# Pairwise products of 32 fields on one core: output slots planned as a ring beside the tiles, upper fields first, a group's load in two pieces

## The chip, the core and the metric

The kernel runs on one core of one Trainium2 chip. The metric is the device time of that core in microseconds. Three runs of the kernel before gave a median of 1286.29 us (1286.14 to 1286.42). Beside them stands one execution under the hardware profiler, from which all rows of the profile come.

## The reference

```python
r_x: float32 (4096, 32, 64)          # batch, fields, embedding
W:   float32 (64, 64)
vid = einsum('bfd,de->bfe', x, W)
i, j = triu_indices(32, k=1)         # 496 pairs i < j
y = x[:, i, :] * vid[:, j, :]        # (4096, 496, 64)
```

Each field of each row of the batch is multiplied by one small matrix, and then, for each of the 496 pairs of fields, the raw left field is multiplied element by element by the transformed right field. The output has 520 MB, the input 33.6 MB.

## The kernel before, in words

**Tiles.** The host lays the batch out as 16 tiles of 256 rows. A tile holds 128 partitions (two halves of the batch tile by 64 embedding places) by 32 fields by 128 columns, so one field of one tile is 512 B in each of 128 partitions, 65,536 B in all, and one output pair has the same size. A *unit* is such a 512 B stretch. One SBUF tensor, `mem`, has 445 units in each partition; input tiles and output slots both live in it. The padding of the DRAM tensors' rows is never moved.

**TensorE.** For each half of a tile's fields (16 of 32) it waits for one count of the semaphore `free`, makes 4 matmuls of 512 columns against a block-diagonal copy of W (each shows as two in the profile) into PSUM (`vid`), and adds one to `there` (function `half`, L272). All tiles' products go into the same PSUM tensor, so a half may be overwritten only when VectorE has done with it; VectorE tells that by `free`.

**VectorE.** For each tile it runs through the 496 pairs in the order of `by_block` (L51): the 120 pairs inside the lower 16 fields, the 256 pairs of a lower with an upper field, the 120 pairs inside the upper fields. The order is cut into instructions by `products` (L67), where a pair run hits the end of an output slot or a seam in it. One instruction is one `tensor_tensor` multiply (L253) of 1 to 112 pairs. It adds one to `made`, or, where a half of PSUM has become free, one to `free` instead (L246 to L248); `owed` holds such a count back if the instruction ends a slot. What an instruction must wait for is worked out in `after` (L164): every transfer that reads units which it overwrites, and, for transfers, the count of `made` at which the last instruction that touched the units has ended. L178 puts that count down; for an instruction that tells `free` it is the next count of `made`.

**Slots.** `SLOTS` is a list written out by a planner: 70 slots of (pairs, first unit in `mem`, seams). The pairs of all 16 tiles, 7936 in one sequence, fill one slot after the other. A slot can span two tiles. When its last pair is made, its store is issued (L264). A seam is a place at which the ground under the slot becomes free at a different time; instructions are cut there.

**Transfers.** All go through SP's one queue, in the order in which the Python code issues them, each with its own semaphore: 11 loads and 70 stores. SP waits before it issues: a store for `made`, a load for the stores and the products that use its units.

**Loads.** Tile 0 comes first in two pieces, with W in front of its lower half. Then tiles 1 to 3 in one transfer and tiles 5 and 4 in two. `GROUPS` has two further groups, tiles 6 to 10 and 15 to 11, each of 160 fields in three pieces (`CUTS`), placed by `XPLACE`. L265 issues the next group's load when `t + 2 == loaded`: at the end of tile 4 for tiles 6 to 10, at the end of tile 9 for tiles 11 to 15. The first store after a group of loads also waits until the second-last piece has landed (`hold[-2]`, L261).

**TensorE's loops.** Tiles of a load run in one hardware loop; ahead of it TensorE waits for the load.

Of the kernel before, what the change touches and what calls it, by code (L numbers as in the profile page):

```python
# [12 lines left out]
C = 128  # L13

UNITS = 445


GROUPS = [
    [[0], [1, 2, 3], [5, 4]],
    [[6, 7, 8, 9, 10]],  # L20
    [[15, 14, 13, 12, 11]],
]
CUTS = [[None, [(0, 38), (38, 64)]], [(0, 127), (127, 134), (134, 160)], [(33, 160), (26, 33), (0, 26)]]
XPLACE = [317, 349, 381, 413, 32, 0, 285, 317, 349, 381, 413, 128, 96, 64, 32, 0]


SLOTS = [
# [10 lines left out]
]  # L38


PAD = 24
# [9 lines left out]
def by_block():  # L51


    def within(lo):
        yield "step", lo, 2, 1, 0
        for k in range(2):
            yield "step", lo, 4, 2, k
        for i in (lo, lo + 8):
            yield "row", i + 4, i, 4, 4
        yield "row", lo + 8, lo, 8, 8  # L60

    yield from within(0)
    yield "row", 16, 0, 16, 16
    yield from within(16)


def products(blocks, at=0):  # L67
# [60 lines left out]
        return instruction  # L128


def overlap(a, b):
    return a[0] < b[1] and b[0] < a[1]


def pairwise_bilinear_kernel(nc, x0, x, out):
    NT = sum(len(tiles) for group in GROUPS for tiles in group)
    F = x0.shape[1] - 1 - PAD0
    D = P // 2
    NP = F * (F - 1) // 2
    BANK = 512 // C  # L140
# [16 lines left out]
    def transfer(out_, in_, units, reads, needs):  # L157
        sem = nc.alloc_semaphore(f"moved{len(moved)}")
        sp.issue(lambda: nc.sync.dma_start(out=out_, in_=in_), needs).then_inc(sem, 16)  # L159
        sp.note(sem, 16)  # L160
        moved.append((units, reads, sem))
        return sem

    def after(units):  # L164

        needs = [(s, 16) for u, reads, s in moved if reads and overlap(u, units)]
        last = max((n for spans, n in worked if any(overlap(units, s) for s in spans)), default=0)
        return needs + [(made, last)] * (last > 0)
# [3 lines left out]
    def work(make, spans, needs, tells):  # L172
# [5 lines left out]
        worked.append((spans, counts[made] + (tells is free)))  # L178
        dve.note(tells, counts[tells])

    place = XPLACE[0]
    first = [
        transfer(
            mem[:, :, :].rearrange("p u c -> p (u c)")[:, place * C - D : (place + HALF) * C],
            x0.rearrange("p u c -> p (u c)")[:, C - D : (1 + HALF) * C],
            (place - 1, place + HALF), False, [],
        ),
        transfer(mem[:, place + HALF : place + F, :], x0[:, 1 + HALF : 1 + F, :], (place + HALF, place + F), False, []),
    ]
    work(lambda: nc.vector.memset(w2[:, :], 0.0), [], [], made)  # L190
    for half in (slice(0, D), slice(D, P)):
        work(
            lambda: nc.vector.tensor_copy(w2[half, half], mem[half, place - 1, C - D :]),  # L193
            [(place - 1, place)], [(first[0], 16), (made, 1)], made,
        )
    nc.vector.wait_ge(made, 3).then_inc(free, 1)
    nc.vector.wait_ge(first[1], 16).then_inc(free, 1)
    owed = 0

    loads = {0: first}  # L200
    loaded = 1

    def load(tiles, cuts):
        nonlocal loaded
        place = XPLACE[tiles[0]]
        at = (loaded - 1) * F
        loaded += len(tiles)
        sems = []
        for lo, hi in cuts or [(0, len(tiles) * F)]:
            units = (place + lo, place + hi)  # L210
            sems.append(transfer(mem[:, units[0] : units[1], :], x[:, at + lo : at + hi, :], units, False, after(units)))
        for t in tiles:
            loads[t] = sems
        return sems

    hold = []
    groups, cuts = iter(GROUPS), iter(CUTS)
    for tiles, parts in zip(next(groups)[1:], next(cuts)):
        hold = load(tiles, parts)

    for t in range(NT):
        xs = (XPLACE[t], XPLACE[t] + F)
        xt = mem[:, xs[0] : xs[1], :]
        blocks = list(products(by_block(), t * NP))
        for k, (at, m, w, i, di, j, dj) in enumerate(blocks):
            slot = bisect_right(STARTS, at) - 1
            n = m * w
            begin, end = STARTS[slot], STARTS[slot + 1]
            size, home = SLOTS[slot][:2]
            units = (home + at - begin, home + at - begin + n)  # L230
            ot = mem[:, home : home + size, :]
            o = mem[:, units[0] : units[1], :]
            if m == 1:
                left = xt[:, i : i + w, :]
                right = vid[:, j : j + 1, :].to_broadcast([P, w, C])
            else:
                o = o.rearrange("p (m w) c -> p m w c", m=m)
                right = vid[:, j : j + (m - 1) * dj + 1 : dj, :].unsqueeze(2).to_broadcast([P, m, w, C])
                if di == 0:
                    left = xt[:, i : i + w, :].unsqueeze(1).to_broadcast([P, m, w, C])  # L240
                else:
                    left = xt.rearrange("p (m d) c -> p m d c", d=di)[:, i // di : i // di + m, i % di : i % di + w, :]
            top = j + (m - 1) * dj
            low = top < HALF
            later = blocks[k + 1 : k + 2]
            owed += not later or low and later[0][5] + (later[0][1] - 1) * later[0][6] >= HALF  # L246
            tells = free if owed and at + n < end else made
            owed -= tells is free  # L248
            needs = [(there, 2 * t + 2 - low), *after(units)]
            if tells is free and t == 0:  # L250
                needs += [(s, 16) for s in loads[1]]
            work(
                lambda: nc.vector.tensor_tensor(o, left, right, ALU.mult),  # L253
                [units, (xs[0] + i, xs[0] + i + w + (m - 1) * di)],
                needs,
                tells,
            )
            at += n
            if at == end:
                needs = [(made, counts[made])]  # L260
                if hold:  # L261
                    needs.append((hold[-2], 16))
                    hold = []
                transfer(out[:, begin:end, :], ot, (home, home + size), True, needs)  # L264
        if t + 2 == loaded < NT:  # L265
            (tiles,) = next(groups)
            hold = load(tiles, next(cuts))

    for sem, n in sp.waits([(sem, 16) for _, _, sem in moved]):
        nc.sync.wait_ge(sem, n)  # L270
# [1 line left out]
    def half(xt, lo):  # L272
        nc.tensor.wait_ge(free, 1).then_inc(free, -1)  # L273
        for b in range(lo, lo + HALF, BANK):
            last = nc.tensor.matmul(vid[:, b : b + BANK, :], lhsT=w2[:, :], rhs=xt(b), start=True, stop=True)  # L275
        last.then_inc(there, 1)

    pe = Queue(nc.tensor, behind)
    runs = []
    for t in range(NT):  # L280
        step = XPLACE[t] - XPLACE[t - 1] if t else 0
        if runs and (t == 1 or loads[t] is loads[runs[-1][-1]]) and (len(runs[-1]) == 1 or step == XPLACE[runs[-1][1]] - XPLACE[runs[-1][0]]):
            runs[-1].append(t)
        else:
            runs.append([t])
    for run in runs:
        base = XPLACE[run[0]]
        if run[0]:
            for s, n in pe.waits([(s, 16) for s in loads[run[0]]]):
                nc.tensor.wait_ge(s, n)  # L290
        if len(run) == 1:
            for lo in (0, HALF):
                half(lambda b: mem[:, base + b : base + b + BANK, :], lo)
            continue
        step = XPLACE[run[1]] - base
        with nc.Fori(0, len(run), engines=[mybir.EngineType.PE]) as i:
            for lo in (0, HALF):
                half(lambda b: mem[:, bass.ds(i * step + (base + b), BANK), :], lo)
    ctx.close()


# [41 lines left out]
```

## Time and profile before

| | before |
|---|---|
| median of three runs | 1286.29 us (1286.14 to 1286.42) |
| the profiled execution | 1286.44 us, of which its span 1284.9 us |
| moved by DMA | 33.59 MB read, 520.09 MB written, 431 GB/s over the span |
| VectorE busy | 1084.1 us, 348 instructions, 345 of them products |
| TensorE busy | 187.7 us, 256 matmuls |
| VectorE idle ahead of products, until a store had landed | 163.4 us, 34 times |
| VectorE idle ahead of products, until TensorE was done | 7.1 us, once |

The span is the time between the first and the last instruction or event of the profiled execution; what lies around it, 1.54 us, is in the run's time and not in the trace. The page divides the span into 40 slices and gives for each the share of time in which the 16 DMA engines were busy, and the rate. The granted clock of TensorE has a mean of 0.57 in this execution.

### The profile page before, as it was taken

The numbers are of one execution on the slowest core, as the hardware profiler recorded it, in microseconds if no ns is written. First come the engines' busy times: TensorE is split into PE (matmuls) and PEld (weight loads), VectorE is DVE, ScalarE is ACT, GpSimd is POOL, SyncE is SP. The second block draws the span as 40 slices with busy tenths as digits, with TensorE's granted clock in tenths as the row PEclk, the third lists the DMA queues.
The fourth block names the chain that finished last, engine by engine and source line by source line (L and its number), as shares of the span: only waits on it lengthen the run. The fifth ranks groups of instructions, "written<-read, shape, count | busy, mean of one in ns | idle before, by whom it ended". The sixth has DMA issues, their size and how long they took to land.

```text
span 1284.9 us, 1195 instructions
## 1 busy us (share of the span) xinstructions
PE 187.7 (15%) x256; PEld 72.8 (6%) x256; DVE 1084.1 (84%) x348; POOL 0.2 (0%) x4
## 2 busy tenths in 40 slices
PE   3111021201021103021110211011202030212000
PEld 1000000100000001000000100000000010000000
DVE  6899998899967389899799993849998889999952
POOL 0000000000000000000000000000000000000000
PEclk8655555656566656555565555565557565565555
DMA  9999999999999999999999999999999999999998
GB/s 401 438 429 439 436 428 433 436 436 423 445 430 431 424 430 426 441 432 434 439 429 443 431 427 441 419 423 438 441 433 442 418 437 441 429 429 443 436 422 385
DMA packets 11668, 553.72 MB, mean 431 GB/s; under 512 B 1296, under 2 KB 1296, under 8 KB 1552
## 3 DMA queue, kind: packets, MB, share of 16 engines
q1 hardware_dynamic: 11664, 553.69, 99.8%
q14 instruction: 4, 0.03, 0.0%
HBM read 33.59 MB, written 520.09 MB: 431 GB/s over the span
## 4 chain that ended last, share of the span: by engine, by line
DMA 48%; DVE 48%; issue 2%; SPq 0%
DVE mem L253 48%; DMA out_dram<-mem 43%; DMA mem<-in_r_x_dram 5%; SPq L159 0%; SPq L124 0%
## 5 line engine op out<-in xcount | busy, mean ns | idle before, releaser
L253 DVE TENSOR_TENSOR mem<-mem,vid 128x1024 f32<-128x1024 f32 (+17 forms) x345 | 1083.5, 3213 | 170.5 <-DMA out_dram<-mem 163.4
L275 PE MATMUL vid<-mem,w 128*128 x256 | 187.7, 902 | 999.8 <-PEq L273 999.8
L275 PEld LDWEIGHTS vid<-mem,w 128*128 128x128 f32 x256 | 72.8, 299 | 1113.7 <-issue 1113.7
L193 DVE COPY w<-mem 64x64 f32<-64x64 f32 x2 | 0.4, 191 | 4.9 <-DMA mem<-in_r_x_dram 4.9
L190 DVE MEMSET w<- 128x128 f32 x1 | 0.2, 165 | 0.8 <-PEq L312 0.8
L312 POOL MEMSET const-bfloat16-1.0<- 128x1 bf16 x1 | 0.1, 102 | 0.0
L312 POOL MEMSET const-uint8-127<- 128x1 uint8 x1 | 0.1, 102 | 0.0
L312 POOL MEMSET const-float32-0.0<- 128x1 f32 x1 | 0.1, 99 | 0.2 <-issue 0.2
L312 POOL MEMSET const-float32-1.0<- 128x1 f32 x1 | 0.1, 99 | 0.0
## 6 DMA issues: line engine op xcount, KB each, us to landing
out_dram<-mem SPq DMA_DIRECT2D x15, 8128.0 KB, 27.5
out_dram<-mem SPq DMA_DIRECT2D x14, 7680.0 KB, 24.9
out_dram<-mem SPq DMA_DIRECT2D x6, 7168.0 KB, 26.2
out_dram<-mem SPq DMA_DIRECT2D x5, 7936.0 KB, 28.3
out_dram<-mem SPq DMA_DIRECT2D x3, 7424.0 KB, 22.6
out_dram<-mem SPq DMA_DIRECT2D x3, 5888.0 KB, 21.0
mem<-in_r_x_dram SPq DMA_DIRECT2D x2, 8128.0 KB, 37.9
out_dram<-mem SPq DMA_DIRECT2D x2, 8064.0 KB, 24.9
```

Of the source, the lines that this page charges most:

```text
L190: work(lambda: nc.vector.memset(w2[:, :], 0.0), [], [], made)
L193: lambda: nc.vector.tensor_copy(w2[half, half], mem[half, place - 1, C - D :]),
L253: lambda: nc.vector.tensor_tensor(o, left, right, ALU.mult),
L275: last = nc.tensor.matmul(vid[:, b : b + BANK, :], lhsT=w2[:, :], rhs=xt(b), start=True, stop=True)
L312: nc = _bacc.Bacc("TRN2", target_bir_lowering=False, num_devices=1, dynamic_dma_scratch_size=512)
```

## The change

The tiles now lie in units 0 to 192 of `mem`, downwards from `TOP`: the first tile of a group ends at unit 192, each further one lies 32 units lower (`place_of`). Slots lie beside and over the used tiles, in units 48 to 440, and were planned anew: 69, of up to 128 pairs (32 of them have 128; before 127 at most), with other places and seams. In a tile the pairs inside the upper 16 fields come first, then those across, then those inside the lower 16; TensorE makes the upper half first, and W stands behind the upper half of tile 0. Each group is loaded in two pieces (128 and 32 fields), so there are 8 loads and 69 stores, 77 transfers. The load of a group is now issued at the start of the group's first tile (before tile 6 and before tile 11). TensorE waits ahead of a group's loop for the pieces that hold the group's first tile; for the others VectorE waits, ahead of the instruction that gives TensorE its `free`.

```diff
+TOP = 192
 GROUPS = [
-    [[0], [1, 2, 3], [5, 4]],
-    [[6, 7, 8, 9, 10]],
-    [[15, 14, 13, 12, 11]],
+    (0, [(32, 160), (0, 32)]),
+    (6, [(64, 192), (32, 64)]),
+    (11, [(64, 192), (32, 64)]),
 ]
-CUTS = [[None, [(0, 38), (38, 64)]], [(0, 127), (127, 134), (134, 160)], [(33, 160), (26, 33), (0, 26)]]
-XPLACE = [317, 349, 381, 413, 32, 0, 285, 317, 349, 381, 413, 128, 96, 64, 32, 0]
...
+    (128, 304), (127, 192, 112), (113, 319), (64, 192), (96, 256, 63), (88, 352), (112, 192), (120, 304, 48),
...
+    (128, 192, 120), (120, 320), (72, 192), (96, 264, 56), (80, 360), (112, 192), (128, 304), (128, 160),
...
-    yield from within(0)
-    yield "row", 16, 0, 16, 16
     yield from within(16)
+    yield "row", 16, 0, 16, 16
+    yield from within(0)
...
+def place_of(t, fields):
+    first = max(begin for begin, _ in GROUPS if begin <= t)
+    return TOP - (t - first + 1) * fields
...
+    def load(g):
+        (begin, pieces), end = GROUPS[g], ends(NT)[g]
+        begin = max(begin, 1)
+        low = place_of(end - 1, F)
         sems = []
+        for lo, hi in pieces:
+            at = (begin - 1) * F + lo - low
+            sems.append(transfer(mem[:, lo:hi, :], x[:, at : at + hi - lo, :], (lo, hi), False, after((lo, hi))))
+            loads.append((range(begin, end), (lo, hi), sems[-1]))
         return sems
...
     for t in range(NT):
+        if t in begins[1:]:
+            hold = load(begins.index(t))
...
-            top = j + (m - 1) * dj
-            low = top < HALF
+            high = j >= HALF
             later = blocks[k + 1 : k + 2]
-            owed += not later or low and later[0][5] + (later[0][1] - 1) * later[0][6] >= HALF
+            owed += not later or high and later[0][5] < HALF
             tells = free if owed and at + n < end else made
             owed -= tells is free
-            needs = [(there, 2 * t + 2 - low), *after(units)]
-            if tells is free and t == 0:
-                needs += [(s, 16) for s in loads[1]]
+            needs = [(there, 2 * t + 2 - high), *after(units)]
+            if tells is free and t + 1 < NT and t + 1 not in begins:
+                needs += loaded(t + 1)
...
-        if t + 2 == loaded < NT:
-            (tiles,) = next(groups)
-            hold = load(tiles, next(cuts))
...
+    for begin, end in zip(begins, ends(NT)):
+        if begin:
+            for s, n in pe.waits(loaded(begin)):
+                nc.tensor.wait_ge(s, n)
```

The lines of the changed kernel that the prediction names: L188 puts down the count of `made` at which an instruction's units are free, L231 issues a group's load, L257 chooses between `free` and `made`, L264 is the product.

More of the change, by code (lines that the diff above doesn't have):

```diff
@@ L60, in within @@
         yield "row", lo + 8, lo, 8, 8
+    yield from within(16)
+    yield "row", 16, 0, 16, 16
     yield from within(0)
-    yield "row", 16, 0, 16, 16
-    yield from within(16)
 def products(blocks, at=0):
@@ L128, in issue, with ends @@
         return instruction
+def place_of(t, fields):
+    first = max(begin for begin, _ in GROUPS if begin <= t)
+    return TOP - (t - first + 1) * fields
+def ends(tiles):
+    return [begin for begin, _ in GROUPS[1:]] + [tiles]
 def overlap(a, b):
@@ L135, in pairwise_bilinear_kernel @@
 def pairwise_bilinear_kernel(nc, x0, x, out):
-    NT = sum(len(tiles) for group in GROUPS for tiles in group)
     F = x0.shape[1] - 1 - PAD0
+    NT = (x.shape[1] - PAD) // F + 1
     D = P // 2
@@ L179, in work @@
         dve.note(tells, counts[tells])
-    place = XPLACE[0]
+    place = place_of(0, F)
     first = [
         transfer(
-            mem[:, :, :].rearrange("p u c -> p (u c)")[:, place * C - D : (place + HALF) * C],
-            x0.rearrange("p u c -> p (u c)")[:, C - D : (1 + HALF) * C],
-            (place - 1, place + HALF), False, [],
+            mem[:, :, :].rearrange("p u c -> p (u c)")[:, (place + HALF) * C : (place + F) * C + D],
+            x0.rearrange("p u c -> p (u c)")[:, HALF * C : F * C + D],
+            (place + HALF, place + F + 1), False, [],
         ),
-        transfer(mem[:, place + HALF : place + F, :], x0[:, 1 + HALF : 1 + F, :], (place + HALF, place + F), False, []),
+        transfer(mem[:, place : place + HALF, :], x0[:, :HALF, :], (place, place + HALF), False, []),
     ]
@@ L192, in pairwise_bilinear_kernel @@
         work(
-            lambda: nc.vector.tensor_copy(w2[half, half], mem[half, place - 1, C - D :]),
-            [(place - 1, place)], [(first[0], 16), (made, 1)], made,
+            lambda: nc.vector.tensor_copy(w2[half, half], mem[half, place + F, :D]),
+            [(place + F, place + F + 1)], [(first[0], 16), (made, 1)], made,
         )
@@ L198, in pairwise_bilinear_kernel, with loaded @@
     owed = 0
[L200 to L207, printed above, removed]
-        sems = []
[L209 to L213, printed above, removed]
-        return sems
[L216 to L219, printed above, removed]
+    loads = [(range(1), (place, place + F + 1), sem) for sem in first]
+    def load(g):
+        (begin, pieces), end = GROUPS[g], ends(NT)[g]
+        begin = max(begin, 1)
+        low = place_of(end - 1, F)
+        sems = []
+        for lo, hi in pieces:
+            at = (begin - 1) * F + lo - low
+            sems.append(transfer(mem[:, lo:hi, :], x[:, at : at + hi - lo, :], (lo, hi), False, after((lo, hi))))
+            loads.append((range(begin, end), (lo, hi), sems[-1]))
+        return sems
+    def loaded(t):
+        units = (place_of(t, F), place_of(t, F) + F)
+        return [(sem, 16) for tiles, piece, sem in loads if t in tiles and overlap(piece, units)]
+    hold = load(0)
+    begins = [begin for begin, _ in GROUPS]
     for t in range(NT):
-        xs = (XPLACE[t], XPLACE[t] + F)
+        if t in begins[1:]:
+            hold = load(begins.index(t))
+        xs = (place_of(t, F), place_of(t, F) + F)
         xt = mem[:, xs[0] : xs[1], :]
@@ L278, in pairwise_bilinear_kernel @@
     pe = Queue(nc.tensor, behind)
[L279 to L289, printed above, removed]
-                nc.tensor.wait_ge(s, n)
[L291 to L298, printed above, removed]
+    for begin, end in zip(begins, ends(NT)):
+        if begin:
+            for s, n in pe.waits(loaded(begin)):
+                nc.tensor.wait_ge(s, n)
+        base = place_of(begin, F)
+        with nc.Fori(0, end - begin, engines=[mybir.EngineType.PE]) as i:
+            for lo in (HALF, 0):
+                half(lambda b: mem[:, bass.ds(base + b - i * F, BANK), :], lo)
     ctx.close()
@@ L318 @@
     x = x.reshape(2, NT, C, F, D).transpose(0, 4, 1, 3, 2).reshape(2 * D, NT, F, C)
-    x = x[:, [t for group in GROUPS for tiles in group for t in tiles]]
-    x0 = _np.pad(x[:, 0], ((0, 0), (1, PAD0), (0, 0)))
-    x0[:, 0, C - D :] = _np.concatenate([w, w])
-    x = _np.pad(x[:, 1:].reshape(2 * D, (NT - 1) * F, C), ((0, 0), (0, PAD), (0, 0)))
+    x0 = _np.pad(x[:, 0], ((0, 0), (0, 1 + PAD0), (0, 0)))
+    x0[:, F, :D] = _np.concatenate([w, w])
+    x = x[:, [t for (begin, _), end in zip(GROUPS, ends(NT)) for t in range(end - 1, max(begin, 1) - 1, -1)]]
+    x = _np.pad(x.reshape(2 * D, (NT - 1) * F, C), ((0, 0), (0, PAD), (0, 0)))
     arrays, args = {}, []
```

17 rows, old and new, of the table SLOTS are left out of this document.

## The prediction

> **What bounds the kernel now.** I read the page from the top: busy shares, then the slices of DMA, then the queue.
>
> ```profile
> span 1284.9 us, 1195 instructions
> PE 187.7 (15%) x256; PEld 72.8 (6%) x256; DVE 1084.1 (84%) x348; POOL 0.2 (0%) x4
> DMA  9999999999999999999999999999999999999998
> DMA packets 11668, 553.72 MB, mean 431 GB/s; under 512 B 1296, under 2 KB 1296, under 8 KB 1552
> q1 hardware_dynamic: 11664, 553.69, 99.8%
> ```
>
> The 16 DMA engines are busy 99.8% of the span: DMA is the bound, VectorE (84%) and TensorE (15%) are not. The change moves the same bytes (every product once, every field once), so time can only be won where DMA is slower than its best or idle, and is lost, microsecond for microsecond, wherever DMA runs dry. Next, by stages, the view of windows; its columns are the stretch, its length, busy time of PE, PEld, DVE, POOL, the granted clock, DMA share, GB/s.
>
> ```profile
> 0.00:1.70 1.70, 0.00 (x0) 0.00 (x0) 0.17 (x1) 0.20 (x4) 1.00 0.00 0
> 380.00:388.00 8.00, 3.83 (x5) 1.76 (x6) 4.17 (x3) 0.00 (x0) 0.50 0.91 392
> 388.00:426.00 38.00, 1.81 (x4) 0.46 (x3) 29.99 (x10) 0.00 (x0) 0.59 0.98 419
> 430.00:770.00 340.00, 54.32 (x72) 21.05 (x72) 305.74 (x103) 0.00 (x0) 0.57 1.00 435
> 900.00:1200.00 300.00, 47.82 (x64) 18.43 (x64) 279.49 (x91) 0.00 (x0) 0.57 1.01 435
> 1281.00:1284.50 3.50, 0.00 (x0) 0.00 (x0) 0.00 (x0) 0.00 (x0) 0.50 0.09 37
> 1284.50:1284.90 0.40, 0.00 (x0) 0.00 (x0) 0.00 (x0) 0.00 (x0) 0.50 0.00 0
> ```
>
> Between loads DMA moves 435 GB/s, share 1.00, so one pair (128 partitions x 512 B = 65,536 B) costs 65,536 / 435 = 0.151 us; 128 pairs 19.3 us, 32 pairs 4.8 us. DMA is at rest only for 1.7 us at the start and about 3 us at the end. A group's load comes with no rest: 0.98 of share at 419 GB/s. How before manages that is in the chain of work that ended last (start, length, what):
>
> ```profile
> 355.60 32.00 DMA out_dram<-mem
> ...
> 387.62 0.34 SPq L159
> ...
> 388.01 38.76 DMA mem<-in_r_x_dram
> 426.77 0.02 issue
> 426.79 0.02 SPq L124
> 426.80 0.03 issue
> 426.83 19.28 DMA out_dram<-mem
> 446.11 0.03 issue
> 446.14 12.96 DVE mem L253 x3
> ```
>
> The second group's load is issued at 387.6, behind the 22nd store, after 2464 pairs by the sums of SLOTS. Tile 6, which needs it, begins at pair 2976 (6 x 496): 512 pairs of lead, mostly tile 5. VectorE multiplies tile 5 while the load runs, and at 426.83, when its second-last piece has landed, two finished stores go out at once. That lead is what the change takes away.
>
> **The change part by part: the load's place.** Before, L265 issues a group's load once the tile two short of the loaded ones is done, one whole tile ahead. After, L231 issues it at the start of the tile that reads it. In the built program of the changed kernel SP's order is: store of slot 24, load of 128 fields, load of 32 fields, store of slot 25; and again store of slot 46, two loads, store of slot 47. Slot 25 holds pairs 2935 to 3048: 41 of tile 5 and 72 of tile 6, so it can't go out before tile 6 is multiplied, and tile 6 waits for the load. Slot 47 (5432 to 5552) has 24 pairs of tile 10 and 96 of tile 11. SP issues in order, so nothing else can fill DMA. Prices of the steps in between:
>
> ```profile
> L253 DVE TENSOR_TENSOR mem<-mem,vid 128x2048 f32<-128x2048 f32 x76 | 171.0, 2279 | 24.8 <-DMA out_dram<-mem 24.8
> L253 DVE TENSOR_TENSOR mem<-mem,vid 128x1024 f32<-128x1024 f32 x101 | 117.4, 1212 | 40.2 <-DMA out_dram<-mem 33.1 <-PE vid L275 7.1
> L253 DVE TENSOR_TENSOR mem<-mem,vid 128x5120 f32<-128x5120 f32 x4 | 21.9, 5481 | 7.3 <-DMA out_dram<-mem 7.3
> L253 DVE TENSOR_TENSOR mem<-mem,vid 128x896 f32<-128x896 f32 x2 | 2.2, 1079 | 0.0
> ```
>
> A product of 8 pairs (1024 elements) is 1.21 us, of 16 pairs 2.28, of 40 pairs 5.48, of 7 pairs 1.08.
>
> ```profile
> 5.90 0.41 DVE L193 COPY w<-mem 64x64 f32<-64x64 f32 x2 [4.91 <-DMA mem<-in_r_x_dram]
> 6.69 10.07 PE L275 MATMUL vid<-mem,w 128*128 x16 [6.69 <-PEq L273]
> 13.37 32.33 DVE L253 TENSOR_TENSOR mem<-mem,vid 128x1024 f32<-128x1024 f32 x10 [7.06 <-PE vid L275]
> 88.28 5.11 PE L275 MATMUL vid<-mem,w 128*128 x8 [52.93 <-PEq L273]
> 432.06 5.59 PE L275 MATMUL vid<-mem,w 128*128 x8 [42.25 <-PEq L273]
> ```
>
> Half a tile on TensorE takes 5.1 us (at 88.28) to 6.7 (6.69 to 13.37, from rest); after a rest of over 100 us I take 6.3 with the hand-over to VectorE. From landing to TensorE's start lies between the 0.02 us with which SP follows a landing (426.77) and the 0.79 from 5.90 to 6.69, which contains two copies; I take 0.5.
>
> ```profile
> 0.73 0.38 SPq L159
> ```
> ```profile
> mem<-in_r_x_dram SPq DMA_DIRECT2D x1, 1056.0 KB, 5.1
> ```
>
> From an issue to its first packet: the first load is issued at 0.73 and DMA moves nothing until 1.7, so 1.0 us. From the last packet to its landing: 0.4, the dead end of the span. Together 1.4; the whole 1056 KB load takes 5.1 us against 2.5 for its bytes at 435 GB/s, so at most 2.6. I take 1.4 and keep 2.6 for the range.
>
> By the Trainium skill, page "DMA: Bandwidth & Descriptors", section "Anatomy of one DMA — SWDGE (gpsimd) path", the fixed part of a DMA is about 2.0 us, most of it the receipt of the last write. It is stated for GpSimd's queue, and this trace shows 1.4 to 2.6 for SP's; by it the four turnarounds below would cost 0.6 us more each, an estimate of 1324.
>
> *Stop A, tile 6.* The load's first piece lands; 0.5 to TensorE, 6.3 for the upper half, then 72 pairs in six products of 8, 8, 8, 16, 16, 16: 3 x 1.21 + 3 x 2.28 = 10.5. With 1.4 that is 18.7 us, while DMA has 32 pairs left: 4.8. DMA rests **13.9 us**.
>
> *Stop B, tile 11.* The second piece (fields 32 to 64) overwrites tile 10, and must wait for its last reader. That product tells its end on `free` (L257), so L188 puts down the next count of `made`, 204, and in the built program it is tile 11's first product that makes 204. So the second piece waits for the first to land, for TensorE and for one product: 1.4 + 0.5 + 6.3 + 1.2 = **9.4 us** with nothing in the queue. Behind it stands slot 47's store, which needs five more products (8, 8, 16, 16, 40): 2 x 1.21 + 2 x 2.28 + 5.48 = 12.5, against the piece's 4.8. Both ends have the same issue delay: another **7.7 us**.
>
> **The ring.** In the new plan a slot may lie on the ground of the one just before, which has to land first: by comparing places this is so twice. The last 15 of slot 24's pairs (8 and 7) and the last 8 of slot 46's. There the queue holds nothing behind the store being waited for: 1.4 + 1.21 + 1.08 = **3.7 us**, and 1.4 + 1.21 = **2.6 us**. Before has one such place (slot 44 on 43), with the third group's load queued between the two. For the other slots: a pair costs VectorE 0.13 us (2279 - 1212 ns for 8 pairs more) and each product 0.15, against 0.151 a pair for DMA, so VectorE gains back about 1.5 us a slot of 128 pairs in five products and a stop isn't followed by others.
>
> **Order of fields, fewer pieces.** Upper half first: 376 of a tile's 496 pairs read the upper products (j of 16 and over), 120 the lower, before as after; TensorE refills one half in 5 to 7 us behind at least 16 us of products on the other. Nothing; without that cover 6 us a tile. VectorE has 314 products for 345: 31 x 0.15 = 4.6 us off an engine that doesn't bound. DMA: 8 loads for 11. In before, the stretch from 380 to 426 loses 8 x (1 - 392/435) + 38 x (1 - 419/435) = 2.2 us against 435 GB/s, twice 4.4 in all. Part is the mixing of loads and stores, which stays: between 0 and 4.4 gained, I take 1.5. At the start the same five microseconds lead to the first product; the first store, 48 pairs, goes behind a 32-field piece (4.8 us; before 26 fields), and 144 pairs are multiplied about 21 us after 13.4, before that store ends. Nothing.
>
> ```profile
> out_dram<-mem SPq DMA_DIRECT2D x15, 8128.0 KB, 27.5
> ```
>
> **Rows of 64 KiB.** 32 stores and 3 loads have rows of 65,536 B, none had before (127 pairs at most). The nearest rows are the 15 stores of 127 pairs (8128 KB), inside the 435 GB/s windows: nothing. Bound on the other side: 419 GB/s as in the load stage.
>
> **Sum.** 13.9 + 9.4 + 7.7 + 3.7 + 2.6 - 1.5 = 35.8 us on the span of 1284.9: 1320.7. Around its span the profiled execution has 1286.44 - 1284.9 = 1.54: 1322.2, and it lies 0.15 over the median of the runs (1286.29): **1322**.
>
> **The rivals.**
> *Faster: DMA never runs dry.* Place: the two group changes. It decides by whether finished stores of 120 pairs (18.7 us) stand behind the load, as two did at 426.83. Price: no stop, the pieces' 0 to 4.4 us gained, about 1284. For it: 84% of VectorE, and before's own load. Against it: SP's order above leaves no finished store behind the load. Chance 0.04. By the same page and section, at 2.0 us a transfer, four transfers fewer would give 8 us, an estimate of 1278; this trace has packets back to back (share 1.00), which speaks against it.
> *Stop A hidden.* Place: tile 6 alone. It decides by whether slot 25's 113 pairs are multiplied before the load's last piece has gone by, 72 of them in 4.8 us. Price: 13.9 us less, 1308. Against it: ten and a half microseconds of products and 6 of TensorE stand in the way. Chance 0.04.
> *64 KiB rows at 419 GB/s.* 35 transfers of 19.3 us, 4% longer each: 26 us more, 1348. It would show in windows with no load. Chance 0.07.
> *The change doesn't do what it says:* the slots don't fit the free ground and VectorE waits at each; then small dips all over, 1335 to 1350. Chance 0.03.
>
> **How the numbers follow.** Forecast 0.82. Its own range: TensorE 5.1 to 6.7 in two stops (-2.4, +0.8), landing to TensorE (-1, +0.6), the pieces (-2.9, +1.5), turnaround up to 2.6 in four stops (+4.8): 1316 to 1329.7. The rivals lie outside with 0.18. Range 1315 to 1330. Faster 0.02, same 0.02 (within 0.2%, 2.6 us, about what measurements of this kernel can tell apart), slower 0.96.
>
> **What would show it.** In the changed profile: DMA's share below 99.8%, about 97%; dips in two places alone, from about 457 us (2808 pairs and 193 fields at 0.151, and 5 for the start) and about 875 us (5304 pairs, 353 fields, and 18 for the first stops); one VectorE wait of about 40 us for TensorE at tile 6 (19.1 and 19.3 of slot 24's store and the load, 7.2 to the first product, less 6 for 41 pairs) and one like it at tile 11, before 7.1 us in all; GB/s of 435 elsewhere. It is wrong if DMA stays at 99% or more, if no such waits are there, if dips stand at other slots, or if 128-pair stores land below 430 GB/s.

## The result, and the profile after

| | before | after |
|---|---|---|
| median of five runs | 1286.29 us (1285.09 to 1288.42) | 1323.28 us (1322.10 to 1324.38) |
| profiled execution, its span | 1286.44, 1284.9 us | 1323.91, 1322.6 us |
| ratio after / before | | 1.029, 95% interval 1.0279 to 1.0301 |

The change makes the kernel 37 us slower; 1322 was forecast. The page of the changed kernel:

```profile
span 1322.6 us, 1291 instructions
PE 180.3 (14%) x256; PEld 70.3 (5%) x256; DVE 1082.9 (82%) x317; POOL 0.2 (0%) x4
DMA  9999999999999896999999999988799999999999
DMA packets 11092, 553.72 MB, mean 419 GB/s; under 512 B 1232, under 2 KB 1232, under 8 KB 1232
q1 hardware_dynamic: 11088, 553.69, 97.2%
```

The same bytes, and 97.2% instead of 99.8% of DMA's time. In the row of digits the 8 and the 6 stand in slices 14 and 16 (33.1 us each, 430 to 463 and 496 to 529), the 8, 8 and 7 in slices 27 to 29 (860 to 959): two dips, where the groups change. A *rest* below is a time in which the DMA engines have nothing to move. The windows cut to the rests, and two others (start:end, length, busy time of PE, PEld, DVE, POOL, granted clock, DMA share, GB/s):

```profile
456.70:461.30 4.60, 0.00 (x0) 0.00 (x0) 3.11 (x4) 0.00 (x0) 0.50 0.24 99
505.90:519.40 13.50, 5.94 (x13) 2.26 (x11) 10.96 (x7) 0.00 (x0) 0.75 0.03 13
878.30:880.90 2.60, 0.00 (x0) 0.00 (x0) 2.04 (x2) 0.00 (x0) 0.50 0.00 0
920.70:930.40 9.70, 8.49 (x14) 3.70 (x15) 2.19 (x2) 0.00 (x0) 0.67 0.00 0
936.30:942.30 6.00, 0.00 (x0) 0.00 (x0) 6.00 (x2) 0.00 (x0) 0.50 0.00 0
100.00:450.00 350.00, 45.48 (x64) 17.73 (x64) 312.85 (x90) 0.00 (x0) 0.57 1.00 435
520.00:860.00 340.00, 47.87 (x64) 18.50 (x64) 306.13 (x85) 0.00 (x0) 0.57 1.00 432
```

Length times what is missing of the share: 3.5, 13.1, 2.6, 9.7 and 6.0, in all 34.9 us, in the five places that the prediction names. From 100 to 450 and from 520 to 860 the share is 1.00. What VectorE does meanwhile shows in its timeline (start, length, what, idle before and who ended it) at tile 6, then at tile 11; the product is L263 in this kernel, not L264:

```profile
458.19 7.81 DVE L263 TENSOR_TENSOR mem<-mem,vid 128x1024 f32<-128x1024 f32 x4 [3.83 <-DMA out_dram<-mem]
508.44 18.74 DVE L263 TENSOR_TENSOR mem<-mem,vid 128x1024 f32<-128x1024 f32 x8 [42.43 <-PE vid L282]
```
```profile
878.86 4.49 DVE L263 TENSOR_TENSOR mem<-mem,vid 128x1024 f32<-128x1024 f32 x2 [2.80 <-DMA out_dram<-mem]
928.21 30.60 DVE L263 TENSOR_TENSOR mem<-mem,vid 128x1024 f32<-128x1024 f32 x10 [44.87 <-PE vid L282]
```

At 458.19 it makes the last pairs of slot 24, whose ground has just become free (the first rest), finishes tile 5 and then waits 42.43 us for tile 6's product, which needs the load. TensorE and SP in the same stretch:

```profile
502.21 9.63 PE L282 MATMUL vid<-mem,w 128*128 x16 [112.30 <-PEq L280]
```
```profile
460.44 0.33 SPq L169 DMA_DIRECT2D out_dram<-mem  x1
460.82 1.39 SPq L169 DMA_DIRECT2D mem<-in_r_x_dram  x2
518.54 0.34 SPq L169 DMA_DIRECT2D out_dram<-mem  x1
880.49 49.31 SPq L169 DMA_DIRECT2D mem<-in_r_x_dram  x2
```

The store and the two loads go out at 460.4 to 462.2, and nothing more until 518.54, when slot 25 is full. What was queued has gone by at 505.9, and the second rest lasts from there until that store begins to move, at 519.4. In the last line, at tile 11, the two loads lie 49 us apart: the second piece goes out only when tile 11's first product is made. The chain of work that ended last shows the same stage:

```profile
921.91 6.28 PE vid L282 x8
928.19 0.02 issue
928.21 13.29 DVE mem L263 x6
941.50 0.02 issue
941.51 19.56 DMA out_dram<-mem
```

Before, the chain went from store to store by way of VectorE; here, at tile 11, TensorE's 6.28 us and six products stand in it.

### The profile page after: what moved, and what is told of

It is laid out like the page before. It is cut to its first block, busy times and chain, and to the rows that moved or that the text cites. A ratio compares the mean times of both kernels' runs of the same rounds, so it can differ in the third digit from the quotient of the medians.

```text
span 1322.6 us, 1291 instructions
## 1 busy us (share of the span) xinstructions
PE 180.3 (14%) x256; PEld 70.3 (5%) x256; DVE 1082.9 (82%) x317; POOL 0.2 (0%) x4
## 3 DMA queue, kind: packets, MB, share of 16 engines
q1 hardware_dynamic: 11088, 553.69, 97.2%
## 5 line engine op out<-in xcount | busy, mean ns | idle before, releaser
L263 DVE TENSOR_TENSOR mem<-mem,vid 128x1024 f32<-128x1024 f32 (+9 forms) x314 | 1082.4, 3518 | 198.2 <-DMA out_dram<-mem 103.8
L282 PE MATMUL vid<-mem,w 128*128 x256 | 180.3, 871 | 1045.6 <-PEq L280 1045.6
## 6 DMA issues: line engine op xcount, KB each, us to landing
out_dram<-mem SPq DMA_DIRECT2D x5, 6656.0 KB, 24.3
```

## The experiments

The theory: DMA rests because the load is issued at the tile that reads it, so that no finished store stands behind it, and because two slots lie on the ground of the one just before. Its rivals: the ring of slots, the 64 KiB rows or the order of fields cost the time; or the time that a wait takes up is not the time that is won without it. In what follows the *path* is the way from the landing of a load's piece over TensorE and the products to the next store that is ready, and the *cover* is the transfer time of what is queued behind that piece. Each ratio is of the experiment's runs to those of the kernel before on the same chip.

**E1, the load moved ahead by one store.**

```diff
-    def load(g):
+    def load(g, only=None):
         (begin, pieces), end = GROUPS[g], ends(NT)[g]
+        pieces = only or pieces
...
-        if t in begins[1:]:
-            hold = load(begins.index(t))
+        if t == 11:
+            load(2, [(32, 64)])
...
             if at == end:
+                if slot == 24:
+                    load(1)
+                if slot == 46:
+                    load(2, [(64, 192)])
```

> The changed kernel, but the second group's load is issued ahead of slot 24's store instead of behind it, and the third group's first piece ahead of slot 46's store; the last piece (fields 32 to 64) stays at the start of tile 11. Ring, slots, order of fields and pieces are those of the change. Theory (DMA runs dry because no finished store stands behind the load): all five rests go, since the store of slot 24 or 46 (19 us) and the first pairs cover the path over TensorE; 1285 to 1289, DMA share over 99.5%, VectorE still waits some 20 us at each group. Rival (the ring of slots, the 64 KiB rows or the order of fields cost the time): at most the waits for TensorE get shorter, 1310 or more. Rival (stop A alone hidden): 1308.

Measured: 1285.76 us (1285.55 to 1286.38), ratio 1.0001 (0.9991 to 1.001). All of the loss is gone. Slots, rows, order of fields and pieces are those of the change. One thing more differs: the moved loads don't set `hold`, so the store behind them doesn't wait until a piece has landed. In the changed kernel that wait is not the one that ends last: TensorE starts at 502.21, so the piece has landed by then, and the store goes out at 518.54. Lines of the page, two windows over the group changes, its waits, and VectorE at the end of slot 24:

```profile
span 1284.8 us, 1292 instructions
q1 hardware_dynamic: 11088, 553.69, 99.9%
```
```profile
457.00:507.00 50.00, 9.02 (x16) 3.74 (x16) 21.61 (x11) 0.00 (x0) 0.60 0.99 423
878.00:930.00 52.00, 9.89 (x16) 4.05 (x16) 35.78 (x12) 0.00 (x0) 0.57 0.97 421
```
```profile
DVE mem L264 <- DMA out_dram<-mem: 111.8, 37, 13.5
DVE mem L264 <- PE vid L287: 49.3, 3, 24.3
```
```profile
458.08 7.82 DVE L264 TENSOR_TENSOR mem<-mem,vid 128x1024 f32<-128x1024 f32 x4 [3.98 <-DMA out_dram<-mem]
```

VectorE still waits up to 24.3 us for TensorE, and that costs nothing: a finished store covers it. Nor does its wait of 3.98 us for the ground of slot 24's last pairs cost anything here: in the changed kernel the same wait, 3.83 us, is the first rest, while here the load stands in the queue meanwhile. So the moved load takes away the two rests of the ring too. The rivals that put the time on rows, order or the ring by itself fall, as far as 0.1%. Nor does it beat the kernel before: DMA is at its bound in both.

**E2, the last piece no longer behind tile 11's first product.**

```diff
+    spare = ctx.enter_context(nc.sbuf_tensor([P, 1], F32))
...
+            if t == 11:
+                work(lambda: nc.vector.memset(spare[:, :], 0.0), [], [], made)
             hold = load(begins.index(t))
```

> The changed kernel with one more VectorE instruction ahead of the third group's load, a memset of one column that tells made, so that the last piece of that load no longer waits for tile 11's first product. Theory: the two rests of stop B are one path (landing, TensorE, six products) less 4.8 us of the last piece, so the first rest (10 us) goes and the second grows from 6 to about 16; time within 1 us of the changed kernel, 1322 to 1324. Rival (the wait for count 204 has a price of its own, 9.4 us as the prediction's term reads): 1314.

Measured: 1322.69 us (1322.30 to 1323.99), ratio 1.029 (1.0273 to 1.0307), as the changed kernel. Its third-group loads on SP, and its window:

```profile
879.44 3.25 SPq L170 DMA_DIRECT2D mem<-in_r_x_dram  x2
```
```profile
924.30:940.90 16.60, 5.87 (x13) 2.23 (x11) 14.12 (x7) 0.00 (x0) 0.81 0.00 0
```

Both pieces now go out within 3.25 us (in the changed kernel within 49.31), and there is one rest of 16.6 us instead of 9.7 and 6.0: the rest behind the piece grows by what was won ahead of it. The wait for count 204, under which the prediction has its 9.4 us, is worth nothing by itself: the store of slot 47 waits for the same TensorE half and the same products with it and without it.

**E3, no slot on the ground of the one just before.**

```diff
-    (128, 304), (127, 192, 112), (113, 319), (64, 192),
+    (128, 304), (112, 192), (128, 304), (64, 192),
...
-    (128, 192, 120), (120, 320), (72, 192),
+    (120, 192), (128, 312), (72, 192),
```

> The changed kernel with two cuts between slots moved: slots 24 and 25 are 112 and 128 pairs instead of 127 and 113, slots 46 and 47 are 120 and 128 instead of 128 and 120, on the same ground, so that no slot overlaps the one just before. Theory: the two rests ahead of these stores (4.3 and 2.8 us by the changed kernel's trace) go, the others stay within 1 us; 1316 to 1318. Rival (VectorE just waits later, and the rest comes back behind the load): 1322 to 1324.

Measured: 1316.28 us (1314.79 to 1316.55), ratio 1.0233 (1.0216 to 1.025): 7.0 us less than the changed kernel. Its windows, the first and the third over the places of the two rests:

```profile
450.00:462.00 12.00, 0.00 (x0) 0.00 (x0) 8.13 (x4) 0.00 (x0) 0.50 0.98 426
498.00:511.90 13.90, 6.37 (x14) 2.43 (x12) 10.93 (x7) 0.00 (x0) 0.87 0.02 7
860.00:885.00 25.00, 0.00 (x0) 0.00 (x0) 15.30 (x6) 0.00 (x0) 0.50 1.03 446
911.30:921.20 9.90, 8.47 (x13) 3.67 (x14) 1.71 (x2) 0.00 (x0) 0.62 0.00 0
927.40:933.60 6.20, 0.00 (x0) 0.00 (x0) 6.20 (x2) 0.00 (x0) 0.50 0.00 0
```

The two rests are gone and the other three are where they were, at 13.6 (13.9 x 0.98), 9.9 and 6.2. So in the changed kernel these two terms have a price of their own: 3.5 and 2.6 by the windows, 7.0 in time (6.4 against E2, which ran on the same chip). They have it only as long as the load stands behind them: E1 keeps the slots and has no such rest.

**E4, the late load alone, in the kernel before.**

```diff
-        if t + 2 == loaded < NT:
+        if t + 1 == loaded < NT:
```

> The kernel before with one edit: a group's load is issued at the end of the tile that precedes the group, one tile later than there, as the change has it; ring, slots, pieces and order of fields of before. Theory (the lead of the load alone): DMA rests at both groups, about 12 us ahead of the store of slot 26 (24 pairs of tile 6 in it), 11 and 24 us at the third group (112 pairs of tile 11 in slot 49), and 4 us ahead of slot 25's; 1330 to 1342. Rival (the new ring or the rows are at fault): 1286 to 1292.

Measured: 1335.31 us (1334.53 to 1336.01), ratio 1.0383 (1.0366 to 1.04). Its rests, then VectorE ahead of slot 44's store, first in this kernel, then in the kernel before:

```profile
419.10:423.00 3.90, 0.00 (x0) 0.00 (x0) 3.90 (x2) 0.00 (x0) 0.50 0.00 0
499.30:510.90 11.60, 9.59 (x16) 3.90 (x16) 4.37 (x4) 0.00 (x0) 0.74 0.05 23
823.80:833.90 10.10, 0.00 (x0) 0.00 (x0) 9.50 (x2) 0.00 (x0) 0.50 0.00 0
933.20:956.60 23.40, 9.36 (x16) 3.81 (x16) 16.35 (x10) 0.00 (x0) 0.72 0.00 0
```
```profile
824.40 26.55 DVE L253 TENSOR_TENSOR mem<-mem,vid 128x8192 f32<-128x8192 f32 x5 [10.46 <-DMA out_dram<-mem]
809.12 26.54 DVE L253 TENSOR_TENSOR mem<-mem,vid 128x8192 f32<-128x8192 f32 x5 [10.45 <-DMA out_dram<-mem]
```

With the old slots, order and rows the late load alone costs 49 us, more than the whole change. The longest rest, 23.4 us, is that of the slot with most pairs of the waiting tile (112). Two of the four rests, 3.9 and 10.1 us, lie well ahead of the load, and TensorE does nothing in them: slot 23 lies on ground of slot 21, slot 44 on ground of slot 43, and VectorE must wait until that has been stored (10.46 us at slot 44). The expectation puts the first of them at slot 25. The kernel before has the same wait, 10.45 us, and no rest, because its load is in the queue meanwhile. So an early load covers two things, the path over TensorE and the waits for ground.

**E5 and E6, how much must stand behind the load.** E1 with slots 24 and 25 cut into three on the same ground, and the load ahead of the middle one (E5; E6 has 96, 32 and 112):

```diff
-    (128, 304), (127, 192, 112), (113, 319), (64, 192),
+    (128, 304), (64, 192), (64, 256, 48), (112, 320), (64, 192),
...
-                if slot == 24:
+                if slot == 25:
...
-                if slot == 46:
+                if slot == 47:
```

The last of these edits keeps the third group's load where E1 has it; the slots behind the new one are numbered one higher.

> E1's kernel with slots 24 and 25 cut anew on the same ground into 64, 64 and 112 pairs, and the second group's load issued ahead of the middle one: 64 finished pairs stand behind the load instead of 127. Theory (a rest is the path from the landed piece to the next ready store, less what stands behind that piece): path about 18.7 us, cover 32 and 64 pairs (4.8 and 9.7), a rest of 4 us ahead of the 112-pair store and nowhere else; E1 and 4: 1288.5 to 1291. Rival (any finished store behind the load is enough): 1285 to 1287.

> The same with 96, 32 and 112 pairs: 32 finished pairs behind the load. Theory: 4.8 us less cover than with 64, so a rest of 9 us; 1293 to 1296. Rival (any finished store is enough): 1285 to 1287; rival (all or nothing, as one waits for the whole load): the 18 us of the changed kernel's first stage, 1303.

Measured: E5 1290.09 us (1289.79 to 1290.44), ratio 1.0035 (1.0021 to 1.005); E6 1295.17 (1294.88 to 1296.13), ratio 1.0078 (1.0061 to 1.0094). The rests, first of E5, then of E6:

```profile
501.30:504.60 3.30, 0.00 (x0) 0.00 (x0) 3.30 (x3) 0.00 (x0) 0.66 0.00 0
```
```profile
501.20:509.70 8.50, 0.89 (x3) 0.06 (x1) 8.50 (x5) 0.00 (x0) 0.86 0.15 66
```

From 64 to 32 pairs of cover the time grows by 5.1 us; 32 pairs are 32 x 0.151 = 4.8 us of transfer. By the windows the rest is 13.1 us in the changed kernel with no store behind the load, 7.2 (8.5 x 0.85) with 32 pairs, 3.3 with 64, and none in E1 with 127. So a rest is the path less the cover, neither "any store will do" nor all or nothing.

**E7, one stage alone.** The changed kernel with the second group's load ahead of slot 24's store and the third group's where the change has it:

```diff
-        if t in begins[1:]:
-            hold = load(begins.index(t))
+        if t == 11:
+            hold = load(2)
...
             if at == end:
+                if slot == 24:
+                    load(1)
```

> The changed kernel with the second group's load ahead of slot 24's store as in E1, and the third group's load where the change has it. Theory: the two rests at tile 6 go (4.3 and 13.6 us), the three at tile 11 stay (2.8, 10 and 6 us); 1303 to 1306. Rival (the stages share a cause, such as a ring that runs low once and stays low): under 1295 or over 1312.

Measured: 1305.24 us (1304.61 to 1305.81), ratio 1.0152 (1.0135 to 1.0169): 18.0 us less than the changed kernel. Its windows, the first stage whole, then the rests of the other:

```profile
440.00:520.00 80.00, 9.09 (x16) 3.75 (x16) 49.09 (x21) 0.00 (x0) 0.56 0.99 424
858.50:861.60 3.10, 0.00 (x0) 0.00 (x0) 0.94 (x1) 0.00 (x0) 0.50 0.00 0
902.40:912.20 9.80, 8.35 (x14) 3.64 (x15) 2.07 (x2) 0.00 (x0) 0.66 0.00 0
918.00:924.20 6.20, 0.00 (x0) 0.00 (x0) 6.20 (x3) 0.00 (x0) 0.50 0.01 3
```

The first stage is whole, the other has its three rests as in the changed kernel, 3.1, 9.8 and 6.2. The losses of the two stages add: 18.0 us for the first, 1305.24 - 1285.76 = 19.5 us for the second, together 37.5; the whole change costs 37.0.

## Why the prediction was right, point by point

- *The bound.* DMA at 99.8% and everything else hidden: the rests came out in the time in all seven experiments, in E1 with none, in E4 with 48.4 us of rests and 49 us of time.
- *Stop A, 13.9 us.* Measured 13.1. Its parts: TensorE's upper half with the hand-over 6.23 (502.21 to 508.44; 6.3 was taken), the six products and the issue 10.1 (508.44 to 518.54; 10.5).
- *Stop B, 9.4 and 7.7 us.* Measured 9.7 and 6.0. The sum was right to 1.4 us. Most of that is the second piece, put at 4.8 us: it held DMA from 930.4 to 936.3, 5.9 us. The account by two terms misleads: the 9.4 stand under the wait for count 204, as if taking that wait away would win them, and E2 shows that it wins nothing. The cost is the path from the landed piece to slot 47's last product less the cover of the second piece, however the two pieces share it.
- *The ring, 3.7 and 2.6 us.* Measured 3.5 and 2.6; E3 took them out alone. That the load's place decides whether they cost anything (E1, E4) the prediction says for the kernel before, but not of these two.
- *Other slots, no further rests.* Right: share 1.00 from 520 to 860, and VectorE made good the loss of a stop without a second one.
- *Fewer pieces, 1.5 us gained: wrong, the mis-sized term of the sum.* E1 has the 77 transfers, the pieces and the rows of the change, and takes 1.0001 of the time before; nothing is gained. The stretch with a load that the prediction had at 419 GB/s stays slow with fewer pieces: E1's two run at 423 and 421. And in the changed kernel DMA's packets took longer, not shorter: all packets of the trace, added up and divided by the 16 engines, take 1282.7 us before, 1285.1 after and 1283.5 in E1.
- *Order of fields, rows of 64 KiB, nothing each.* E1 bounds them together, with the pieces and the ring under an early load: within 0.1%. Single ones weren't tried alone; 128-pair stores fill the windows at 435 GB/s (100 to 450).
- *The turnaround.* 1.4 us was taken. The two short rests bear it out: 2.6 at slot 46 leaves 1.4 beside a product of 1.21, 3.5 at slot 24 leaves 1.2 beside products of 1.21 and 1.08. The Trainium skill, page "DMA: Bandwidth & Descriptors", section "Anatomy of one DMA — SWDGE (gpsimd) path", has about 2.0 us for the fixed part, for GpSimd's queue. On SP's queue the changed kernel's trace has 1.2 to 1.4, and the measurement decides.
- The rivals: *DMA never runs dry* fell with the five rests, and its point of decision was right: E1 fulfils it with 127 pairs of cover and has no loss. *Stop A hidden*, *64 KiB rows* and small dips all over did not come about.
- *The signs.* DMA's share is 97.2% (about 97 was named), the rests begin at 456.7 and 878.3 (457 and 875), and the two waits for TensorE are 42.4 and 44.9 us (about 40).

Of the 37.7 us on the span, 2.4 are packets that took longer (1285.1 - 1282.7), and the other 35.3 are DMA's rests, 34.9 of them in the five windows. The prediction's five rests add up to 37.3, 2.4 more than these; against that it counted 1.5 us of gain that did not come, and no slower packets. That the sum came within 1.3 us of the median is therefore in part luck: the mechanism and each rest are right to 1.7 us, and the errors happen to cancel.

## What to carry to other kernels

Where a single in-order queue is the bound, look at what is queued behind a load, not at how busy the engines are: the rest is the path from the landing of the piece that is waited for to the next finished store, less the transfer time of what stands behind that piece. A prefetch therefore has to be placed by the transfers ahead of it *and behind it*. Here moving each load ahead by one store (127 and 128 pairs) was worth all of the 37 us; with 64 pairs behind one of the loads the time was 4.3 us over E1, with 32 pairs 9.4. A load in the queue also covers a wait for ground that would otherwise be a rest. A wait on the way to the same end has no price of its own until it is the last to end, so remove one and look before you add up waits.

## What the runs showed of the hardware

DMA's packets are a little slower in a stretch that follows a rest. By the windows, the changed kernel moves 435 GB/s before its first rest (100 to 450) and 432 behind it (520 to 860), and E1, which has no rest there, moves 435 in the same stretch, but 433 in its last one:

```profile
520.00:860.00 340.00, 49.78 (x64) 19.23 (x64) 306.95 (x88) 0.00 (x0) 0.55 1.01 435
943.00:1280.00 337.00, 46.19 (x64) 17.99 (x64) 288.90 (x79) 0.00 (x0) 0.57 1.00 433
```

The packets themselves tell more than these rates. A row of 65,536 B is one packet, and its median time over the three stretches between the group changes is:

| kernel | first stretch | behind tile 6 | behind tile 11 |
|---|---|---|---|
| E1, no rest | 2418 ns | 2418 ns | 2420 ns |
| changed, E2 and E3, rests at both | 2418 ns | 2422 ns | 2422 ns |
| E5 and E6, a rest at tile 6 alone | 2418 ns | 2422 ns | 2418 ns |
| E7, rests at tile 11 alone | 2418 ns | 2418 ns | 2422 ns |

So a packet takes 4 ns, 0.2%, longer behind a rest, until the next group change, whether the rest was 3 us (E5) or 13. E1's 2420 without a rest shows that a rest is not the only cause. Why it is so, no run here shows. All packets together take 2.4 us more in the changed kernel than in the kernel before.

Rows of exactly 64 KiB cost no more per byte than rows of 127 pairs: 65,536 B in 2418 ns (the changed kernel's first stretch) and 65,024 B in 2399 ns (the kernel before) are both 27.1 GB/s on one of the 16 engines.
